# A transformer block's output projection: the gated bias put into the token tiles by ScalarE and the tokens added by the load, instead of additions on GpSimd

## The chip, the cores and the metric

One core of one Trainium2 chip. The metric is the device time of one execution in microseconds; the median of a few runs is given with the lowest and the highest.

## The reference

A conditioned transformer block (DiT block) on x of 2 batches x 2048 tokens x 512 channels, in float32. The condition gives six modulation vectors per batch (shift, scale and gate for the attention and for the MLP):

```
mod = silu(cond) @ Wada + bada;  sh_a, sc_a, gt_a, sh_m, sc_m, gt_m = split(mod, 6)
xm = layernorm(x; g1, be1) * (1 + sc_a) + sh_a
x  = x + gt_a * (causal_attention(xm; Wqkv, 16 heads of 32) @ Wproj + bproj)
xm = layernorm(x; g2, be2) * (1 + sc_m) + sh_m
x  = x + gt_m * (gelu(xm @ W1 + b1) @ W2 + b2)
```

The change concerns the third line: x + gt_a * (... @ Wproj + bproj). The kernel multiplies the gate into Wproj and into the bias ahead of time, so what is left is x + gated bias + (attention output @ gated Wproj).

## The kernel before, in words

The kernel runs in stages: keys, queries and values of batch 0; attention of batch 0; output projection of batch 0 (with the first steps of batch 1's normalisation beside it); the same three for batch 1 (with the first steps of the MLP beside the projection); then the MLP in four blocks of 512 tokens, taken two at a time. The matrix products of the linear layers use Strassen-like schemes of seven products, which is why there are many sums of blocks on VectorE and GpSimd.

The engines each have a queue of instructions and work through it in order. Most instructions around the projection are wrapped in `act(...)` or `mm(...)`, which keep them in program order on their engine; DMA issues on SP and a few others (the eviction in L1352 among them) are placed by the scheduler. An engine waits at the head of its queue, and all behind it wait with it.

**The output projection** is `project_phase` (L1302). It takes the 16 token tiles of 128 tokens of a batch in four quarters of 512 tokens, in the order `last_order` = 0, 2, 1, 3; I call the 16 tiles steps 0 to 15, and quarter k = 0 to 3. For each quarter the attention output lies transposed in a tile `at` of four chunks c0 to c3 of 128 channels; it has to be multiplied by the inverse softmax sums (`rbs`) before use. In a step:

- `tokens(n + 6)` makes sure that token tiles up to six ahead are being loaded (SP, L1318). The tiles of steps 0 to 3 were loaded during attention into space borrowed from a key tile (they show as `kst` in the profile), and the bias was added there by GpSimd (L472). The tiles of steps 4 to 15 are `xt`, with six buffers: tile 10 takes the buffer of tile 4, tile 11 that of tile 5, and so on, so a load waits until the store of the tile that had the buffer has read it.
- from quarter 1 on, GpSimd adds the gated bias `bgate` to the token tile (L1345).
- TensorE multiplies the four chunks of `at` by Wproj into a bank `ps_o` (L207 is the line of the helper for all matmuls; a step is 8 of them in the trace). All four chunks are needed for every token tile of the quarter.
- VectorE adds the bank to the token tile (L1352), takes the statistics for the second normalisation (L219, L222), and SP stores the tile as `x1d` (L1354).
- in the first three quarters, GpSimd scales one chunk of the next quarter's `at` (L1358): chunk c0 in the quarter's first step, c3 in its last. So the scalings of the third quarter are spread over steps 4 to 7, and step 8 needs all of them.
- `between(n)` does work for the next stage. In batch 0: statistics and normalisation of batch 1's first tokens (ScalarE L226 and L969, TensorE's transposes, ScalarE's evictions `xmT` in L279), the load of the weights `wqk` from GpSimd's queue (L931, after step 6), sums of them on VectorE and GpSimd (L949). In batch 1: the MLP's first normalisation (`xm`, half of its evictions on ScalarE, L279) and its token sums (L1637).

On SP also lie the loads of `at` (L1327), the path of the last softmax sums (`sum` store L745, `r` load L379, inverted on VectorE L386, `inv` store L387, wide load L393 into `rbs`), loads of pieces of W2 for sums made later (L1246), and in batch 1 the MLP's first weights (`w<-w1d`). The PSUM has six banks for the projection of batch 0 and four for that of batch 1, shared with the transposes.

Of the kernel before, what the change touches and what calls it, by code (L numbers as in the profile page):

```python
# [12 lines left out]
ALU = mybir.AluOpType  # L13
# [14 lines left out]
def dit_block_kernel(  # L28
# [36 lines left out]
    nc = tc.nc  # L65
# [6 lines left out]
    TQ = QB // P  # L72
# [11 lines left out]
    def pool(name, bufs=1, **kw):  # L84
        return tc.tile_pool(name=name, bufs=bufs, reuse_waits="tile", **kw)
# [68 lines left out]
    bgate = bp.tile([P, D], F32, tag="bgate", name="bgate")  # L154
# [46 lines left out]
    def x_rows(n):  # L201
        t0 = (n % NT) * P
        return x[n // NT, t0 : t0 + P, :]

    def mm(*args, **kw):

        return tc.keep_in_program_order(nc.tensor.matmul(*args, **kw))  # L207

    def act(ins):

        return tc.keep_in_program_order(ins)
# [5 lines left out]
    def stats(pool_, xt, n, mv, keep=False):  # L217
        st = pool_.tile([P, 6], F32, tag="stat", name="stat", bufs=2)
        ins = nc.vector.bn_stats(st, xt)  # L219
        if keep:  # L220
            act(ins)
        nc.vector.bn_aggr(mv[:, n, :], st)  # L222

    def inv_std(mv, rstd, shift, lo, hi, keep=False):
        order = act if keep else (lambda ins: ins)
        order(nc.scalar.activation(rstd[:, lo:hi], mv[:, lo:hi, 1], AF.Sqrt, bias=eps))  # L226
        order(nc.vector.reciprocal(rstd[:, lo:hi], rstd[:, lo:hi]))
        order(
            nc.vector.scalar_tensor_tensor(
                shift[:, lo:hi], mv[:, lo:hi, 0], -1.0, rstd[:, lo:hi],  # L230
                ALU.mult, ALU.mult,
            )
        )
# [1068 lines left out]
    def project_phase(row, psum, between):  # L1302

        b = row.b
        with pool(f"proj{b}") as pp:
            n = 0
            ats = list(row.at_s)  # L1310
            rbs = {1: row.rb_s[1], 2: row.old_queries(), 3: row.rb_s[0]}
            rows_x = [b * NT + i * TQ + t for i in last_order for t in range(TQ)]
            xts = list(row.xt_s)

            def tokens(upto):
                while len(xts) < min(upto, NT):
                    xt = pp.tile([P, D], F32, tag="xt", name="xt", bufs=6)
                    nc.sync.dma_start(xt, x_rows(rows_x[len(xts)]))  # L1318
                    xts.append(xt)

            row.load_sums(len(units) - 1, len(units))
            tokens(TQ + 6)
            for k, i in enumerate(last_order):
                if k in (0, 1):

                    at = pp.tile([P, C, QB], F32, tag="at", name="at", bufs=2)
                    nc.sync.dma_start(at, od[b][last_order[k + 2]])  # L1327
                    ats.append(at)
                at = ats[k]
                for t in range(TQ):  # L1330

                    if n == 0:
                        nc.sync.dma_start(rbs[2], wide_d[b][last_order[2]])
                        nc.sync.dma_start(
                            rbs[3][:, : C - 1], wide_d[b][last_order[3]][:, : C - 1]
                        )
                    elif n == 3:
                        row.invert(len(units) - 1, len(units))
                    elif n == 4:
                        row.widen(len(units) - 1, rbs[3][:, C - 1, :])  # L1340

                    tokens(n + 6)
                    nt, xt = rows_x[n], xts[n]
                    if k > 0:
                        act(nc.gpsimd.tensor_tensor(xt, xt, bgate, ALU.add))  # L1345
                    ps = psum.tile([P, D], F32, tag="mm", name="ps_o")
                    for c in range(C):
                        mm(
                            ps, at[:, c, t * P : (t + 1) * P], row.wproj[:, c, :],
                            start=(c == 0), stop=(c == C - 1),  # L1350
                        )
                    nc.vector.tensor_tensor(xt, ps, xt, ALU.add)  # L1352
                    stats(pp, xt, nt, mv2, True)
                    nc.sync.dma_start(x1d[nt], xt)  # L1354
                    if k + 1 < NQ:
                        d = ats[k + 1][:, t, :]
                        act(
                            nc.gpsimd.tensor_tensor(d, d, rbs[k + 1][:, t, :], ALU.mult)  # L1358
                        )
                    between(n)  # L1360
                    n += 1
        if b:
            inv_std(mv2, rstd2, shift2, NT, 2 * NT)
# [170 lines left out]
    with pool("qkv1") as qp, pool("ps_qkv1", bufs=6, space=PSUM) as ps_mm:  # L1534
# [3 lines left out]
        def between(n):  # L1538
            if n == 6:
                qkv.load_w(nc.gpsimd)  # L1540
            if 9 <= n < 12:
                qkv.weight_sum(nc.vector, n - 9)
            elif n == 13:
                qkv.weight_sum(nc.gpsimd, 3)
            if n >= 12:
                qkv.token_sum(0, (S1, S2, S3, A22)[n - 12])

            if n < MTT:
                qkv.stats(0, n, True)
            if n in (5, 8):  # L1550
                qkv.norm(0, n // 8)()
            if n == 8:
                qkv.load_x(1)
            if n >= NT - MTT:
                qkv.stats(1, n - (NT - MTT), True)

        project_phase(past, ps_mm, between)

        def also(g, n):
# [40 lines left out]
    with ExitStack() as mlp:  # L1600
# [104 lines left out]
        def between(n):  # L1705
# [10 lines left out]
            if n == 13:  # L1716
                for k in range(1, 5):
                    token_sum(k)

        project_phase(row, ps_mm, between)  # L1720
        for _ in range(3):
            next_weights()
# [814 lines left out]
```

## Time and profile before

| | |
|---|---|
| runs (3) | median 2240.48 us, 2238.31 to 2241.14 |
| profiled execution | 2238.97 us, its span 2237.2 us |
| granted TensorE clock | 0.999 |
| projection of batch 0 / batch 1 | from about 714 / 1458 us, some 57 to 60 us each |
| token loads (`xt<-in_x_dram`) | 12 in each, 256 KB each, from SP |
| additions of the bias (L1345) | 12 in each, on GpSimd |

In the rows of the profile PE is TensorE's matmuls, PEld its weight loads, DVE VectorE, ACT ScalarE, POOL GpSimd and SPq the issues of SP's DMA queue. A row of a timeline has the start, the duration, engine, line, operation, output<-input, shape and count, and in brackets how long the engine sat idle before and what released it. A row of a group has busy time, the mean in ns, then the idle time before and its releasers. A row of waits has the total, the number of waits and the longest.

### The profile page before, as it was taken

The page shows a single profiled execution, that of the slowest core. Times are in us where ns is not written, and L with a number is a line of the kernel's source. Part 1 is how long each engine was busy: PE and PEld are TensorE (multiplying, and loading weights), DVE is VectorE, ACT ScalarE, POOL GpSimd, SP SyncE. Part 2 cuts the span into 40 slices and gives each one's busy share as a digit, 9 for nine tenths or more (in the row PEclk, how much of TensorE's full clock was granted, in tenths as well). Part 3 has the DMA queues.
Part 4 walks back from the last instruction along what each step waited for, and adds up shares of the span by engine and source line. Part 5 has one row for each costly group of instructions (what it writes and reads, how often), then busy time and mean ns, then how long its engine had stood idle before and what let it go on. Part 6 is the DMA issues. An engine that isn't in the chain of part 4 may idle for free.

```text
span 2237.2 us, 34305 instructions
## 1 busy us (share of the span) xinstructions
PE 2196.1 (98%) x12273; PEld 1470.9 (66%) x12273; DVE 1580.7 (71%) x3373; ACT 1038.0 (46%) x2132; POOL 1458.9 (65%) x903
## 2 busy tenths in 40 slices
PE   7999999999999999999999999999999999999998
PEld 5887555555543588855555555345788888888887
DVE  4578766767757676777677777656586687688587
ACT  4444555655555244355655555703323532532520
POOL 4253998998992696189989898456616616535540
PEclk9999999999999999999999999999999999999999
DMA  8787143232233799542324113376655554654653
GB/s 273 249 278 192 42 89 76 67 86 48 88 111 114 258 311 317 153 105 62 86 67 104 35 52 127 105 243 216 236 181 177 192 173 157 212 183 142 219 158 111
DMA packets 166627, 340.99 MB, mean 152 GB/s; under 512 B 17216, under 2 KB 49516, under 8 KB 164664
## 3 DMA queue, kind: packets, MB, share of 16 engines
q1 hardware_dynamic: 158080, 302.05, 45.0%
q0 software_dynamic: 8000, 36.21, 4.3%
q8 instruction: 97, 1.59, 0.3%
q14 instruction: 74, 0.61, 0.1%
q10 hardware_dynamic: 376, 0.55, 0.1%
HBM read 246.46 MB, written 100.14 MB: 155 GB/s over the span
## 4 chain that ended last, share of the span: by engine, by line
PE 88%; DVE 4%; POOL 3%; DMA 2%; ACT 1%; issue 1%; SPq 0%; DVEq 0%; ACTq 0%; POOLq 0%
PE ps_a L207 23%; PE st L207 18%; PE ps_b L207 14%; PE o L207 10%; PE s L207 9%; PE ps_c L207 4%; PE ps_o L207 4%; PE sm L207 3%; DVE junk L503 1%; POOL ee L700 1%; PE ps_xt L215 1%; ACT e L675 1%; DVE mx L509 1%; PE ps_o L215 1%; POOL wqk L949 0%
## 5 line engine op out<-in xcount | busy, mean ns | idle before, releaser
L675 ACT ACTIVATE e<-st 128x512 f32<-128x512 f32 (+1 forms) x1152 | 574.7, 578 | 363.4 <-PE st L207 317.5
L509 DVE TENSOR_REDUCE mx<-s 128x1 f32<-128x512 f32 x576 | 381.7, 686 | 193.9 <-PE s L207 192.9
L700 POOL TENSOR_TENSOR ee<-ee,e 128x2048 f32<-128x2048 f32 x106 | 485.9, 4584 | 10.2 <-ACT e L675 4.3
L207 PE MATMUL st<-qst,kst 128*128 128x512 f32 (+3 forms) x1280 | 408.8, 386 | 0.0
L207 PE MATMUL s<-kst,qst 128*128 128x512 f32 (+3 forms) x1046 | 380.6, 395 | 6.0 <-DVE mx L509 3.7
L207 PE MATMUL ps_a<-sum,w 128*128 128x256 f32 (+1 forms) x1304 | 335.6, 391 | 3.1 <-DVE sum L1637 2.9
L207 PE MATMUL o<-e,vv 128*32 128x512 f32 (+3 forms) x2560 | 293.2, 537 | 0.3 <-POOL e L687 0.3
L207 PEld LDWEIGHTS st<-qst,kst 128*128 128x128 f32 x1280 | 228.5, 188 | 97.5 <-issue 65.7
L207 PEld LDWEIGHTS ps_a<-sum,w 128*128 128x128 f32 x1304 | 246.2, 190 | 44.3 <-issue 6.6
L503 DVE CUSTOM_DVE_ANT_0 junk<-s,causal 128x128 bf16<-128x128 f32 (+3 forms) x470 | 220.8, 470 | 61.2 <-PE s L207 47.4
L207 PEld LDWEIGHTS s<-kst,qst 128*128 128x128 f32 x1046 | 194.9, 188 | 71.0 <-DVE mx L509 17.0
L700 POOL TENSOR_TENSOR ee<-e 128x2048 f32<-128x2048 f32 x42 | 192.5, 4584 | 43.0 <-ACT e L675 43.0
L207 PE MATMUL ps_b<-sum,w 128*128 128x256 f32 (+1 forms) x744 | 186.8, 382 | 0.0
L2228 POOL TENSOR_TENSOR h<-h,h 128x512 f32<-128x512 f32 x96 | 119.4, 1274 | 69.8 <-DVE h L1734 69.8
L207 PEld LDWEIGHTS <-sel 32*128 32x128 bf16 x1152 | 29.6, 91 | 197.5 <-issue 196.6
L207 PEld LDWEIGHTS ps_b<-sum,w 128*128 128x128 f32 x744 | 140.4, 190 | 22.5 <-issue 2.6
L509 DVE TENSOR_REDUCE mx<-st 128x1 f32<-128x512 f32 x192 | 131.1, 683 | 0.5
L687 POOL TENSOR_SCALAR_AFFINE_SELECT e<-e 128x512 f32<-128x512 f32 x128 | 83.2, 669 | 68.1 <-ACT e L675 68.1
L1799 POOL TENSOR_TENSOR sum<-xm 128x256 f32<-128x256 f32 x22 | 23.2, 1054 | 154.3 <-PE ps_a L207 154.3
L207 PEld LDWEIGHTS o<-e,vv 128*32 128x32 f32 x2560 | 59.1, 108 | 92.3 <-issue 73.2
L207 PE MATMUL st<-fold,sel 32*128 32x512 bf16 (+1 forms) x1152 | 117.7, 372 | 1.4
L1071 POOL TENSOR_TENSOR lo<-lo,hi 128x512 fp32r<-128x512 f32 x32 | 40.7, 1274 | 105.7 <-ACT hi L1069 100.7
(263 smaller groups left out, 3580.4 us busy)
## 6 DMA issues: line engine op xcount, KB each, us to landing
w<-w1x SPq DMA_DIRECT2D x42, 896.0 KB
qst<-q SPq DMA_DIRECT2D x128, 256.0 KB
kst<-k SPq DMA_DIRECT2D x128, 256.0 KB
w<-w2d SPq DMA_DIRECT2D x28, 1024.0 KB
w<-w2d SPq DMA_DIRECT2D x28, 768.0 KB
q<-hi SPq DMA_DIRECT2D x32, 256.0 KB
q<-lo SPq DMA_DIRECT2D x32, 256.0 KB
k<-hi SPq DMA_DIRECT2D x32, 256.0 KB
```

The lines of the kernel that those rows point to most:

```text
L207: return tc.keep_in_program_order(nc.tensor.matmul(*args, **kw))
L215: return tc.keep_in_program_order(nc.tensor.transpose(dst, src, ident[:n, :n]))
L503: nc.vector.tensor_tensor_reduce(junk[:, :w], x, causal[:, QB - w :], 1.0, MASKED, ALU.add, ALU.max, m,)
L509: self.vector(nc.vector.tensor_reduce(m, x, axis=AX.X, op=ALU.max))
L675: act(nc.scalar.activation(e4[:, h, :w], sts[h][:, :w], AF.Exp))
L687: nc.gpsimd.affine_select(d, d, pattern=[[0, HC], [1, P]], compare_op=ALU.is_ge, fill=0.0, base=0, channel_multiplier=-1,)
L700: act(nc.gpsimd.tensor_tensor(dst, x, y, ALU.add))
L1071: engine.tensor_tensor(lo, d, hi.bitcast(F32), ALU.subtract)
L1799: act(engine.tensor_tensor(dst, u, v, ALU.subtract))
L2228: act(engine.tensor_tensor(d[j], d[j], x[j], ALU.add))
```

## The change

```
             def tokens(upto):
                 while len(xts) < min(upto, NT):
                     xt = pp.tile([P, D], F32, tag="xt", name="xt", bufs=6)
-                    nc.sync.dma_start(xt, x_rows(rows_x[len(xts)]))
+                    act(nc.scalar.copy(xt, bgate))
+                    act(
+                        nc.gpsimd.dma_start(
+                            xt, x_rows(rows_x[len(xts)]), accum_op=ALU.add
+                        )
+                    )
                     xts.append(xt)
 
             row.load_sums(len(units) - 1, len(units))
-            tokens(TQ + 6)
+            tokens(TQ + 4)
...
-                    tokens(n + 6)
+                    tokens(max(n + 4, TQ + 4))
                     nt, xt = rows_x[n], xts[n]
-                    if k > 0:
-                        act(nc.gpsimd.tensor_tensor(xt, xt, bgate, ALU.add))
```

A token tile of steps 4 to 15 is now made in two steps: ScalarE copies the gated bias into it, and a DMA issued from GpSimd's queue loads the tokens and adds them onto what is there. The addition on GpSimd goes, and so does the load from SP. Four tiles are started ahead of the first step, where six were, and in step n those up to tile n + 3 instead of n + 5. Copies and loads are kept in program order on ScalarE and on GpSimd. The order of instructions on TensorE and VectorE stays the same; on SP, the scheduler puts some DMAs in another order.

## The prediction

> **What bounds the kernel now.** I read the page first (busy time, chain), then the stretches of the two projections, then who TensorE waits for in them.
>
> ```profile
> PE 2196.1 (98%) x12273; PEld 1470.9 (66%) x12273; DVE 1580.7 (71%) x3373; ACT 1038.0 (46%) x2132; POOL 1458.9 (65%) x903
> ...
> PE 88%; DVE 4%; POOL 3%; DMA 2%; ACT 1%; issue 1%; SPq 0%; DVEq 0%; ACTq 0%; POOLq 0%
> ```
>
> TensorE is busy for 2196.1 of 2237.2 us, and 88% of the chain is TensorE. POOL's 65% says nothing yet: the changed stage has to be looked at by itself.
>
> ```profile
> 730.00:740.00 10.00, 10.00 (x31) 4.83 (x30) 5.19 (x13) 5.03 (x9) 6.03 (x5) 1.00 0.98 343
> 740.00:750.00 10.00, 9.66 (x29) 4.53 (x28) 5.60 (x11) 1.93 (x4) 9.98 (x11) 1.00 1.01 348
> ...
> 1475.00:1485.00 10.00, 10.00 (x37) 5.41 (x36) 6.87 (x12) 1.13 (x2) 9.84 (x8) 1.00 0.77 249
> ```
>
> The columns after the stretch are its length, then busy time of PE, PEld, DVE, ACT, POOL, then granted clock, DMA share and GB/s. In both projections TensorE is full at clock 1.00, even where POOL is full too (9.98, 9.84). ScalarE is nearly idle. One gap is left, 0.34 us in 740 to 750. The waits of TensorE from 700 to 800 and its timeline name it:
>
> ```profile
> PE ps_o L207 <- POOL at L1358: 0.3, 1, 0.3
> ```
> ```profile
> 742.56 2.74 PE L207 MATMUL ps_o<-kst,at 128*128 128x512 f32 x6
> 745.63 1.12 PE L207 MATMUL ps_o<-kst,at 128*128 128x512 f32 x2 [0.34 <-POOL at L1358]
> ```
>
> This is the first token tile (step 8 of 16, counting from 0) of the third quarter. It needs all four scaled chunks of its attention output, and GpSimd ends the fourth scaling only then. In the second projection TensorE waits for nothing. So the most that the change can remove here is 0.34 us of 2237.2, 0.015%; the question is what it can add. (About 0.2%, 4.5 us, is what a measurement of this kernel tells from no change.)
>
> **The change part by part.**
>
> *Removed: 24 additions on GpSimd, 24 loads from SP.*
>
> ```profile
> L1345 POOL TENSOR_TENSOR xt<-xt,bgate 128x512 f32<-128x512 f32 x24 | 32.1, 1339 | 30.8 <-DMA xt<-in_x_dram 20.6 <-DVE mv L222 4.7 <-DVE shift L229 2.6
> ```
> ```profile
>   POOL xt L1345: 10.3, 5
>   PE ps_o L207: 6.9, 3
> ```
>
> The first row is 24 x 1.339 = 32.1 us of GpSimd. The other two, from what VectorE sat idle for before it evicted the projection's banks in the first batch, say that VectorE waited 10.3 us for these additions. Both lie beside a full TensorE: six PSUM banks let VectorE lag. If that cover were gone, up to 10.3 us would be at stake; it is not gone, as the 0.34 us above is TensorE's only wait. Worth on the path: the addition between two scalings in the gap's chain, below.
>
> *Added on ScalarE: 24 copies of 128x512 from SBUF.* No such copy is in the trace; the bounds are the eviction copy (0.590) and the normalisation from SBUF (0.807).
>
> ```profile
> L744 ACT COPY sums<-sm 128x512 f32<-128x512 f32 x32 | 18.9, 590 | 8.6 <-PE sm L207 8.6
> L969 ACT ACTIVATE x<-x,shift,rstd 128x512 f32<-128x512 f32 x28 | 21.4, 807 | 6.2 <-DVE shift L229 5.1 <-ACT lo L1064 0.6 <-DMA q<-hi 0.6
> ```
>
> 24 x 0.59 to 0.81 = 14 to 19 us, on an engine busy 1.93 of 10 us in the stage. I take 0.7. What matters is the queue: from tile 10 on, the first that reuses one of the six buffers, a copy waits until the store out of that buffer has landed, and behind it on ScalarE stand the evictions of transposed tiles.
>
> *Added on GpSimd: 24 accumulating loads to issue.* The trace has no accumulating transfer. The nearest are plain issues on the same queue:
>
> ```profile
> L1278 POOL DMA_DIRECT2D w2d<-kst x10: 540/557/575, 796.8 to 887.4; - x10
> ```
> ```profile
> L931 POOL DMA_DIRECT2D wqk<-in_L_cond_Wqkv_dram x4: 722/731/790, 740.1 to 742.3; - x4
> ...
> DMA to landing us min/median/max: 6.3/8.7/10.5
> ```
> ```profile
> L1828 POOL DMA_DIRECT2D w1x<-w x4: 947/952/952, 1543.6 to 1594.5; - x4
> ```
>
> One run per partition costs 0.557, two 0.731, more 0.952. The new loads have one run per partition but a second operand: I take I = 0.73 and keep 0.55 to 0.95 (and, as a rival, far more). An addition of 1.27 thus gives way to about 0.73 on the same queue: GpSimd gains, unless an issue waits for its copy.
>
> *The chain at step 8.* GpSimd's order after the change is, by the compiled order of instructions: four loads, four scalings of the second quarter, scaling c0 of the third, load 8, c1, load 9, c2, four weight loads, load 10, c3. Rows of before:
>
> ```profile
> 736.01 1.90 ACT L279 ACTIVATE xmT<-ps_xt,c,a 128x256 f32<-128x256 f32 x4
> ```
> ```profile
> 738.89 1.27 POOL L1358 TENSOR_TENSOR at<-at,qst 128x512 f32<-128x512 f32 x1
> 740.10 2.96 POOL L931 DMA_DIRECT2D wqk<-in_L_cond_Wqkv_dram  x4
> 743.09 1.28 POOL L1345 TENSOR_TENSOR xt<-xt,bgate 128x512 f32<-128x512 f32 x1
> 744.30 1.27 POOL L1358 TENSOR_TENSOR at<-at,qst 128x512 f32<-128x512 f32 x1
> ```
>
> Copy 9 stands behind the four xmT evictions, which TensorE's transposes time, so it ends at 736.01 + 1.90 + 0.7 = 738.6. Then load 9 (I), c2 1.27, weights 2.96, load 10 (I), c3 1.27: 744.1 + 2I = 745.6 at I = 0.73. Before, c3 ended at 744.30 + 1.27 = 745.57. TensorE is ready at 742.56 + 2.74 = 745.30. So the gap stays: 0.0, with -0.34 at I = 0.55 and +0.4 at 0.95.
>
> *The store that copy 10 waits for.* SP's rows, and SP's own waits from 700 to 790:
>
> ```profile
> 736.64 0.43 SPq L1354 DMA_DIRECT2D x1d<-xt  x1
> ...
> 743.14 0.33 SPq L1318 DMA_DIRECT2D xt<-in_x_dram  x1
> 743.56 0.62 SPq L1354 DMA_DIRECT2D x1d<-xt  x1
> ...
> 752.16 0.34 SPq L1318 DMA_DIRECT2D xt<-in_x_dram  x1
> ```
> ```profile
> SPq L1318 <- DMA x1d<-xt: 21.4, 6, 6.4
> SPq L1246 <- POOL kst L1358: 10.6, 1, 10.6
> ```
> ```profile
> 731.65 0.69 DVE L1352 TENSOR_TENSOR xt<-ps_o,xt 128x512 f32<-128x512 f32 x1 [0.21 <-PE ps_o L207]
> ...
> 757.81 0.68 DVE L1352 TENSOR_TENSOR xt<-ps_o,xt 128x512 f32<-128x512 f32 x1
> ```
>
> Load 10 waited on SP for the store of tile 4, from 736.64 to 743.14, 6.5 us, and load 11 for that of tile 5, 8.6 us; now ScalarE waits. Load 10's turn on GpSimd comes at 738.6 + I + 1.27 + 2.96 = 743.6, so its copy must end by then and the store land by 742.9. The second wait helps: SP was held 10.6 us behind the scalings of the second quarter, because weights for the next stage stood ahead of the softmax sums. In the compiled order other weights go first, the sums leave up to 5 us earlier, and the store of tile 4, evicted at 732.3, can leave at about 733. It lands at 739.5 or, at 8.6, at 741.6: no wait. If it leaves as late as before, it lands at 743.1, the copy ends at 743.8, the load at 744.5 and c3 at 745.8, +0.2; at 8.6 us, +2.3.
>
> *Load 10 and its successors* queue behind the 2 MB of weights, which took up to 10.5 us: 744.3 + 10.5 = 755, against the eviction of tile 10 at 757.8 above. The later copies wait for stores of tiles 5 to 9, each due 3 us or more ahead. *The look-ahead* falls from 6 tiles to 4; tiles 8 and 9 have fresh buffers, so only the store wait comes of it. *Four loads ahead of the second quarter's scalings:*
>
> ```profile
> 714.27 0.59 ACT L744 COPY sums<-sm 128x512 f32<-128x512 f32 x1
> ```
> ```profile
> 713.49 4.93 POOL L1358 TENSOR_TENSOR kst<-kst,qst 128x512 f32<-128x512 f32 x4
> ```
> ```profile
> 714.11 20.87 PE L207 MATMUL ps_o<-kst 128*128 128x512 f32 x48
> ```
>
> Four copies end at 714.9 + 4 x 0.7 = 717.7, the last load at 718.4, the scalings 4.9 later, 723.3. A step is 8 of these matmuls, 3.45 us, so TensorE comes to step 4 at 727.9. Hidden by over 4 us.
>
> *The second projection.* The row that copy 9 stands behind, and step 8's start:
>
> ```profile
> 1482.15 0.56 ACT L279 ACTIVATE xm<-ps_xt,c,a 128x256 f32<-128x256 f32 x1 [0.42 <-DVE xm L274]
> ```
> ```profile
> 1488.27 13.90 PE L207 MATMUL ps_o<-kst,at 128*128 128x512 f32 x32
> ```
>
> Copy 9 ends at 1482.71 + 0.7 = 1483.4; load 9, c2, load 10 and c3 end at 1485.9 + 2I = 1487.4. The fourth chunk is due three quarters of a step after 1488.27, at 1490.9. 3.5 us to spare: nothing.
>
> *Sum:* 0.0 us (-0.34 to +2.3). The profiled execution is 2238.97 (span 2237.2, 1.8 around it); the median of the runs is 2240.48, 1.5 above. I predict the median unchanged: 2240.5, own range 2240.1 to 2242.8 before run spread.
>
> **The rivals.**
>
> *A, slower: the issue of an accumulating load is long.* The gap grows by 2I - 1.47. At I = 2.5 that is +3.5 at step 8; then four loads and four scalings stand between it and step 12, where scalings already stretched in the trace:
>
> ```profile
> 755.69 2.19 DVE L949 TENSOR_TENSOR wqk<-wqk 128x1024 f32<-128x1024 f32 x1
> ```
> ```profile
> 756.77 2.25 POOL L1358 TENSOR_TENSOR at<-at,qst 128x512 f32<-128x512 f32 x1
> ```
>
> A scaling took 2.25 rather than 1.27 beside VectorE's addition from SBUF. Steps 8 and 12 together give about +6: 2246.5. It decides from I = 2.2 (4.5 us); below 1 it is nothing. Against it: every issue in the rows is under 1 us. [...] The trace shows the stretching of scalings, but the plain issues at 740 had VectorE mostly idle beside them. [...] Chance 0.11.
>
> *B, slower: the accumulating transfer itself is slow.* A plain tile moves in 0.7 us by this row (36.21 MB in 4.3% of 2237 us is 376 GB/s):
>
> ```profile
> q0 software_dynamic: 8000, 36.21, 4.3%
> ```
>
> A read and a write of the destination would make it two or three times that. A step is 3.44 us, so it decides above about 4 us a tile; at 6, in order on one queue, the six tiles behind the weights (753) put tile 15 at 789. TensorE ends the stage near 771 and can run some 7 us further on its six banks, so it loses about 10, and as much in the second batch: +20, 2260. Nothing in the trace speaks for a factor of eight. Chance 0.05.
>
> *C, faster:* GpSimd's relief and SP's earlier stores remove more than the gap. TensorE's waits in the stage hold 0.34 us, so this needs later stages to shift as well; their orders of instructions are the same on all engines. 0.34 gives 2240.1, which cannot be told from no change; over 4.5 us, 2235, I can name no row for. Chance 0.05.
>
> *D, the change does nothing because the wait only moves:* GpSimd waits for ScalarE's copy, which waits for the store, as SP's load did. Beyond the forecast's end it goes if the store of tile 4 leaves 1.5 us later than before, behind the weights that now stand just ahead of it on SP, and takes 8.6: c3 ends at 749.4, +3.8, 2244.3. Chance 0.10, mostly within 0.2%.
>
> **How the numbers follow.** Forecast 0.69, A 0.11, B 0.05, C 0.05, D 0.10. Within 0.2%: 0.69 + 0.09 (D's part below 4.5 us) = 0.78; slower: A and B, 0.16, plus 0.01 of D, 0.17; faster 0.05. For 8 in 10 the range spans the runs' own spread below (2238.31) and reaches A's 2246.5 above; B is left out.
>
> **What would show it.** Right: TensorE's only wait in 700 to 800 still at step 8, 0 to 1 us, POOL's issues at 0.5 to 1 us, ScalarE's copies at 0.6 to 0.8 with idle time "<- DMA x1d" before some, SP free of its 10.6 us hold, VectorE's waits for POOL gone, the second projection full. Wrong: issues over 2 us; a tile landing over 10 us after its issue with VectorE waiting for it; a TensorE wait at step 12 or in 1458 to 1525; or the store of tile 4 landing after 745.

## The result and the profile after

| | before | after |
|---|---|---|
| median of 20 runs of each | 2237.93 us (2235.28 to 2241.84) | 2244.82 us (2239.80 to 2251.20) |
| ratio | | 1.0028, 95% interval 1.0020 to 1.0035 |
| profiled execution, its span | 2238.97, 2237.2 us | 2241.53, 2239.8 us |
| mean granted clock of the profiled execution | 0.999 | 0.999 |

The changed kernel is slower, by 6.3 us (4.5 to 7.8) going by the ratio. The profiled executions differ by 2.6 us only, so the profile shown first is one of the milder executions. That gap had to be explained too.

Page of after, engines and the queue of GpSimd's DMAs (packets, MB, share of 16 engines' time):

```profile
PE 2196.7 (98%) x12273; PEld 1469.9 (66%) x12273; DVE 1581.8 (71%) x3373; ACT 1050.9 (47%) x2156; POOL 1448.1 (65%) x903
...
q0 software_dynamic: 11456, 42.50, 6.0%
```

GpSimd is relieved by 10.8 us and ScalarE does 12.9 us more. Nothing in these totals speaks of a loss. It is in TensorE's waits of the two projections, from 700 to 800 and from 1455 to 1530 (total, times, longest):

```profile
PE ps_o L207 <- POOL at L1361: 1.0, 1, 1.0
PE ps_a L207 <- DVE lo L1083: 0.8, 1, 0.8
PE sm L207 <- DVE ee L703: 0.6, 1, 0.6
PE ps_xt L215 <- ACT qst L969: 0.4, 1, 0.4
```
```profile
PE ps_o L207 <- POOL at L1361: 1.7, 1, 1.7
PE sm L207 <- DVE ee L703: 0.6, 1, 0.6
```

The 0.6 us for sm lie ahead of the projections and stand in both lists of before too. Apart from the attention's last waits (sm, and one of 0.2 us), the lists of before held 0.34 us at step 8 of the first projection and none in the second. Now the largest is at step 8 of the second, where the prediction saw 3.5 us to spare. GpSimd, ScalarE and SP there:

```profile
1484.13 0.88 POOL L1320 DMA_DIRECT2D xt<-in_x_dram  x1 [10.06 <-ACT xt L1318]
1484.73 1.57 POOL L1361 TENSOR_TENSOR at<-at,qst 128x512 f32<-128x512 f32 x1
1491.17 0.88 POOL L1320 DMA_DIRECT2D xt<-in_x_dram  x1 [4.86 <-DVE xn L255]
1491.78 1.56 POOL L1361 TENSOR_TENSOR at<-at,qst 128x512 f32<-128x512 f32 x1
```
```profile
1483.22 0.61 ACT L1318 COPY xt<-bgate 128x512 f32<-128x512 f32 x1
1490.26 0.62 ACT L1318 COPY xt<-bgate 128x512 f32<-128x512 f32 x1 [6.42 <-DMA x1d<-xt]
```
```profile
1479.78 0.54 SPq L393 DMA_DIRECT2D qst<-inv  x1
...
1480.94 0.37 SPq L1664 DMA_DIRECT2D w<-w1d  x1
1481.41 0.60 SPq L1357 DMA_DIRECT2D x1d<-xt  x1
```

Read from the bottom: the store of tile 4 leaves SP at 1481.41, behind the inverse softmax sums (L393, held until they had landed) and an 896 KB load of MLP weights. ScalarE's copy 10 waits for it until 1490.26, 8.8 us after its issue. Load 10 follows at 1491.17 and scaling c3 stands behind it. (The page names VectorE's xn as releaser of load 10; that had long been done, and the copy ended at 1490.88.) VectorE had finished the store's tile at 1476.21 + 0.69 = 1476.9, so SP held the store for 4.5 us, and its landing took 8.8 us. Before, c3 came in a run of additions and scalings that nothing held, 11 us ahead of its need, and the store had left 5 us earlier. GpSimd and SP of before:

```profile
1478.48 1.27 POOL L1358 TENSOR_TENSOR at<-at,qst 128x512 f32<-128x512 f32 x1
```
```profile
1476.32 0.31 SPq L1354 DMA_DIRECT2D x1d<-xt  x1
```

**A length for each stage.** Times of whole runs scatter by several us (before's from 2235.28 to 2241.84), from causes outside the two projections too. So each profile below is read by the length of its two projections alone, from the start of the first ps_o matmul to that of the first matmul of the next stage. Rows of after:

```profile
714.37 16.15 PE L207 MATMUL ps_o<-kst 128*128 128x512 f32 x37
...
773.14 1.03 PE L207 MATMUL ps_a<-xmT,wqk 128*128 128x256 f32 x4
...
1458.74 17.43 PE L207 MATMUL ps_o<-kst 128*128 128x512 f32 x40
...
1520.14 1.88 PE L207 MATMUL ps_a<-xm,w 128*128 128x512 f32 x4
```

773.14 - 714.37 = 58.77 us and 1520.14 - 1458.74 = 61.40 us; before 57.39 and 59.43.

| kernel | first projection | second | ratio of times (95%) |
|---|---|---|---|
| before | 57.39 | 59.43 | |
| after | 58.77 | 61.40 | 1.0028 (1.0020 to 1.0035) |
| after, once more (e9) | 58.77 | 65.30 | 1.0035 (1.0022 to 1.0048) |
| eight buffers (e1) | 58.75 | 59.43 | 1.0013 (1.0004 to 1.0021) |
| scaling first (e2) | 57.90 | 59.43 | 1.0007 (0.9999 to 1.0016) |
| change in batch 0 alone (e3) | 58.74 | 59.43 | 1.0013 (1.0004 to 1.0021) |
| change in batch 1 alone (e4) | 57.57 | 65.14 | 1.0023 (1.0015 to 1.0032) |
| plain loads (e5) | 57.70 | 61.09 | 1.0004 (0.9995 to 1.0013) |
| copies alone (e6) | 57.83 | 59.43 | 1.0013 (0.9999 to 1.0026) |
| look-ahead of six (e7) | 69.72 | 70.20 | 1.0117 (1.0102 to 1.0132) |
| additions left out (e8) | 56.79 | 59.43 | 1.0004 (0.9995 to 1.0012) |
| held by 11 additions (e10) | 57.56 | 61.42 | 1.0010 (0.9998 to 1.0021) |
| held by 13 additions (e11) | 57.59 | 66.93 | 1.0034 (1.0021 to 1.0046) |
| both cures (e12) | 57.79 | 59.43 | 1.0008 (0.9997 to 1.0018) |

Where no GpSimd instruction is late the second projection lasts 59.43 us to the hundredth, so each excess there is the price of one stop (in e7, of several).

### The profile page after: what moved, and what is told of

Read it like the earlier page. It is cut to its first block, busy times and chain, and to the rows that moved or that the text cites. A ratio compares the mean times of both kernels' runs of the same rounds, so it can differ in the third digit from the quotient of the medians.

```text
span 2239.8 us, 34319 instructions
## 1 busy us (share of the span) xinstructions
PE 2196.7 (98%) x12273; PEld 1469.9 (66%) x12273; DVE 1581.8 (71%) x3373; ACT 1050.9 (47%) x2156; POOL 1448.1 (65%) x903
## 4 chain that ended last, share of the span: by engine, by line
PE 57%; DVE 2%; POOL 1%; DMA 1%; ACT 0%; issue 0%; SPq 0%; DVEq 0%; ACTq 0%; POOLq 0%
PE ps_a L207 19%; PE ps_b L207 11%; PE st L207 9%; PE o L207 5%; PE s L207 4%; PE ps_c L207 3%; PE ps_o L207 2%; PE sm L207 2%; PE ps_xt L215 1%; POOL ee L700 1%; PE ps_o L215 1%; DVE junk L503 1%; DVE mx L509 0%; DVE y L1737 0%; DVE sum L1640 0%
## 5 line engine op out<-in xcount | busy, mean ns | idle before, releaser
L1071 POOL TENSOR_TENSOR lo<-lo,hi 128x512 fp32r<-128x512 f32 x32 | 40.6, 1273 | 105.4 <-ACT hi L1069 105.3
```

What stands on the lines that cost most here:

```text
L1071: engine.tensor_tensor(lo, d, hi.bitcast(F32), ALU.subtract)
```

## The experiments

Theory W: the loss is the wait of scaling c3, on GpSimd, behind a load that waits through ScalarE's copy for the store of tile 4. Rivals A and B are those of the prediction: a price of each accumulating load, in its issue or in its transfer. Theory G comes from what e4 shows.

**e1, eight buffers.**

```
-                    xt = pp.tile([P, D], F32, tag="xt", name="xt", bufs=6)
+                    xt = pp.tile([P, D], F32, tag="xt", name="xt", bufs=8)
```

> Edit: the changed kernel with eight xt buffers instead of six. Tile 10 then has a buffer of its own, so neither its copy nor its load waits for the store of tile 4; issues, copies, accumulating transfers and all orders of instructions stay. Theory W (the scaling c3 of the third quarter stands on GpSimd behind a load that waits, through ScalarE's copy, for the landing of the store of tile 4): ScalarE's waits for x1d<-xt of 27.8 us mostly go, TensorE's wait at step 8 falls from 1.7 to 0 in the second projection and from 1.0 to at most 0.5 in the first; of the changed kernel's +6.3 us at least 4 go, ratio to the kernel before 1.0000 to 1.0010. Rival A (long issue of an accumulating load, and VectorE's and GpSimd's stretched instructions beside it): the issues are the same, +5 to +6 us stay, ratio 1.0022 or more. Rival B (slow accumulating transfer): the same +5 to +6 stay.

The second projection is back at 59.43 with the issues and the accumulating transfers as they were: its stop hung on that store, and A and B fall there. The first stays at 58.75, and its stop at 1.0 us:

```profile
PE ps_o L207 <- POOL at L1361: 1.0, 1, 1.0
```

So W is wrong for the first batch, and the ratio, 1.0013, misses the expected 1.0010: 3.4 of the 6.3 us went, not 4. What holds c3 in the first batch is told with the prediction's steps, below.

**e2, the scaling ahead of the next tile.**

```
-                    tokens(max(n + 4, TQ + 4))
...
                             nc.gpsimd.tensor_tensor(d, d, rbs[k + 1][:, t, :], ALU.mult)
                         )
+                    tokens(max(n + 4, TQ + 4))
                     between(n)
```

> Edit: the changed kernel with the start of the next token tile moved behind the scaling of the step, so on GpSimd c3 stands ahead of load 10 and not behind it. Six buffers, the copy still waits for the store. Theory W: TensorE's wait at step 8 goes in both projections (0 to 0.4 us), at least 4 of the 6.3 us go, ratio 1.0000 to 1.0010, although ScalarE's waits for x1d<-xt stay. Rival A: c3 ends one issue (0.9 us) earlier and nothing else changes: at most 1.8 us over the two batches, +4.5 stays, ratio about 1.0020. Rival B: the loads come a little later, +6 or more stays, ratio 1.0027 or more.

57.90 and 59.43, no wait at step 8 in either projection, ratio 1.0007: some 4.7 of the 6.3 us gone with copies, accumulating loads, buffers and the store's wait all as in the change. It is the place of c3 in GpSimd's queue that costs. A's 1.0020 and B's 1.0027 lie outside the interval.

**e3 and e4, one batch alone** (the other batch loads from SP and adds on GpSimd, as before).

```
+                    if b != 0:
+                        nc.sync.dma_start(xt, x_rows(rows_x[len(xts)]))
+                        xts.append(xt)
+                        continue
...
+                    if b != 0 and k > 0:
+                        act(nc.gpsimd.tensor_tensor(xt, xt, bgate, ALU.add))
```

> Edit: the change in the projection of batch 0 alone; batch 1 as in the kernel before. From the profiled pair (TensorE's wait at step 8 grew by 0.6 in batch 0 and by 1.7 in batch 1). Theory W, with the second store held longer behind other queue entries: about a quarter to a third of the loss, +1 to +2.5 us, ratio 1.0005 to 1.0011. Rivals A and B (a price of each load): half, +3.1 us, ratio 1.0014.

> Edit: the change in the projection of batch 1 alone; batch 0 as in the kernel before. Theory W: two thirds to three quarters of the loss, +3.8 to +5.3 us, ratio 1.0017 to 1.0024, with a wait of TensorE of 1.5 us or more at step 8 of the second projection. Rivals A and B: half, +3.1 us, ratio 1.0014.

1.0013 and 1.0023, together 1.0036: they add up (e3 lies a little above W's 1.0011), and batch 1 carries some two thirds, as W had it, although the intervals alone do not exclude halves. e4's profile brought what the first one of after lacked: a longer stop, and a slower TensorE behind it. Its timeline of TensorE, and then its ps_o matmuls from 1484 to 1500 (durations min, median, max):

```profile
1492.69 9.69 PE L207 MATMUL ps_o<-kst,at 128*128 128x512 f32 x18 [3.74 <-POOL at L1368]
```
```profile
L207 PE MATMUL ps_o<-kst,at x19: 592/592/1173, 1486.2 to 1499.6; 128*128 128x512 f32 x19
```

After a stop of 3.74 us matmuls take 1.17 us in place of 0.59, and the granted clock is 0.69, 0.50 and 0.95 in the three stretches of 2 us from 1492: (0.31 + 0.50 + 0.05) x 2 / 0.5 = 3.4 us at half clock. Around the stop of 1.7 us in the first profile of after it is 1.00 in all stretches from 1486 to 1500. This is theory G: a stop as long as e4's costs its length and a stretch at half clock behind it, one as short as that of after its length alone. It is the author's estimate from these two profiles.

**e5, plain loads.**

```
                         nc.gpsimd.dma_start(
-                            xt, x_rows(rows_x[len(xts)]), accum_op=ALU.add
+                            xt, x_rows(rows_x[len(xts)])
                         )
```

> Edit: the changed kernel with plain loads from GpSimd's queue in place of the accumulating ones; copies, waits, buffers and every order of instructions stay. The gated bias is thereby left out of the token tiles of steps 4 to 15. Theory W (the store that copy 10 waits for, and c3 queued behind): the issue falls from 0.90 us to 0.56 to 0.73, TensorE's waits at step 8 stay (0.3 to 1.0 us in the first projection, 1.5 to 4 in the second), +4 to +6.5 us stay, ratio 1.0018 to 1.0029. Rival B (the accumulating transfer or its issue is the price): most of the loss goes, at most +2 us, ratio below 1.0010.

Here W lost on the time: 1.0004, below its 1.0018. That is what rival B of this run expected (below 1.0010). Yet W's mechanism stands in the profile, a stop of 1.4 us in the second projection, of 61.09 us:

```profile
PE ps_o L207 <- POOL at L1361: 1.4, 1, 1.4
```

Going by the medians, the accumulation therefore counts for more than W allowed. What it adds is in these rows, of after and of e5, line L1320:

```profile
L1320 POOL DMA_DIRECT2D xt<-in_x_dram x24: 873/902/1867, 715.9 to 1508.4; - x24
...
DMA to landing us min/median/max: 4.0/6.5/11.3
```
```profile
L1320 POOL DMA_DIRECT2D xt<-in_x_dram x24: 537/577/590, 715.6 to 1506.7; - x24
...
DMA to landing us min/median/max: 3.0/4.6/9.4
```

and in the share of GpSimd's DMA queue from 1455 to 1500, of e4 and of e5:

```profile
q0 software_dynamic: 1264, 2.32, 30.6%
```
```profile
q0 software_dynamic: 720, 2.36, 16.7%
```

The issue is 0.90 us in place of 0.58, and the same bytes occupy the 16 DMA engines for 13.8 us in place of 7.5 (30.6% and 16.7% of 45 us), 1.8 times as long. The profiles hold only 1.4 of the some 5 us that e5 gains over after: 58.77 - 57.70 in the first projection and 61.40 - 61.09 in the second. That the transfer makes the store late they do not show: in e5 the inverse sums landed 7.4 us after their issue and the store of tile 4 after 9.0, in after 7.1 and 8.8. The rest of the gain lies in executions without a profile. That fewer of e5's runs have a long stop with half clock behind it (next runs) is suggested by their mean clock, 0.9992 over 11 runs against 0.9979 over 20 of after, though the clock varies for other reasons too (0.9983 in e2, which has no stop). How much of e5's gain is the issue and how much the transfer was not separated.

**e6, copies alone** (into a tile that nobody reads, in the kernel before).

```
                     nc.sync.dma_start(xt, x_rows(rows_x[len(xts)]))
+                    cb = pp.tile([P, D], F32, tag="cb", name="cb", bufs=2)
+                    act(nc.scalar.copy(cb, bgate))
```

> Edit: the kernel before, and beside each of its 24 token loads one copy of the gated bias on ScalarE into a tile that nobody reads: the copies alone, without the wait for a store. Theory W: nothing, ratio 0.9995 to 1.0005. Rival C1 (ScalarE's 24 copies of 0.62 us, or what they do to other engines' SBUF instructions, are a part of the loss): +1 us or more, ratio 1.0005 or more, with TensorE or VectorE waiting for ScalarE's evictions.

1.0013 lies in C1's range, above W's 1.0005, but its interval of 0.9999 to 1.0026 holds both and decides nothing. The stages do: 57.83 and 59.43, so 0.4 us in the first projection, where TensorE waits 0.77 us for GpSimd at step 8 instead of 0.34, and the second is untouched. In neither does TensorE wait for an eviction of ScalarE, which is what C1 needs.

**e7, a larger dose: the old look-ahead.**

```
-            tokens(TQ + 4)
+            tokens(TQ + 6)
...
-                    tokens(max(n + 4, TQ + 4))
+                    tokens(max(n + 6, TQ + 6))
```

> Edit: the changed kernel with the look-ahead of six tiles that the kernel before had (six started ahead, tiles up to n + 5 in step n), buffers still six. Now load 10 stands ahead of scaling c1 of the third quarter, load 11 ahead of c2 and load 12 ahead of c3, and tile 12's copy waits for the store of tile 6. Theory W, a larger dose: c3 ends when the store of tile 6, evicted at about 739 us, has landed 6.5 to 10 us later, plus copy, issue and scaling of about 2.5: 748 to 752 against a need at 745.3; TensorE waits 3 to 7 us at step 8 of each projection and later steps wait too, in all +8 to +20 us, ratio 1.0035 to 1.009. Rivals A and B (a price of each load): the loads are earlier and as many, no more than the changed kernel's +6.3, ratio at most 1.0028.

1.0117, 26 us: over W's 20, and four times what A and B allow. Three scalings now stand behind three such loads, and TensorE waits for them, in the first projection for 9.0 us in all:

```profile
PE ps_o L207 <- POOL at L1361: 9.0, 3, 4.0
```

The stages are 12.3 and 10.8 us longer. In the second, 3.8 us are waits for the scalings and 3.5 us a wait for an eviction (xm, L279) that stands on ScalarE behind a copy held by its store, so the late store reaches TensorE by ScalarE's queue too. The excess over the stops fits theory G: the clock was 0.59 from 750 to 760 and 0.66 from 1510 to 1520.

**e8, the additions left out.**

```
-                    if k > 0:
-                        act(nc.gpsimd.tensor_tensor(xt, xt, bgate, ALU.add))
```

> Edit: the kernel before without its 24 additions on GpSimd, loads from SP as they were: the removal alone, so the most that any way of moving these additions can bring. The gated bias is thereby left out of the token tiles of steps 4 to 15. Theory W with its side observation (GpSimd, relieved, starts its sums of W2 about 3 us earlier beside VectorE's addition L1071, which takes 2.9 us instead of 0.7 and holds TensorE 0.7 us at about 786 us): the 0.34 us at step 8 goes, up to 0.7 us come back later; ratio 0.9995 to 1.0005. Rival C (the additions hold more than TensorE's waits show): 2 us or more faster, ratio below 0.9991.

Even with the additions gone for nothing, the first projection is 0.6 us shorter (56.79), the second the same, and the time 1.0004 (0.9995 to 1.0012). That bounds what any change of this kind could bring here. The side observation fell: TensorE has no wait at 786 us in e8, although GpSimd starts its sums there even earlier (778.0). The addition L1071 beside them takes 1.61 us there and 2.96 in after, so the wait of 0.7 us comes from how the two fall on each other, not from the relief itself.

**e9, the changed kernel again.**

> The changed kernel itself once more, beside the next three on one chip: a second profiled execution, and a second median. [...]

1.0035 and a stop of 3.9 us, more than twice that of the first profile, of the same program. TensorE, then stretches of 2 us of all engines (length, busy time of PE, PEld, DVE, ACT and POOL, then granted clock, DMA share, GB/s):

```profile
1497.89 12.69 PE L207 MATMUL ps_o<-kst,at 128*128 128x512 f32 x25 [3.90 <-POOL at L1361]
```
```profile
1498.00:1500.00 2.00, 2.00 (x4) 0.90 (x5) 0.92 (x2) 0.10 (x1) 1.60 (x2) 0.77 1.04 347
1500.00:1502.00 2.00, 2.00 (x3) 0.67 (x2) 0.65 (x2) 0.62 (x1) 0.71 (x2) 0.50 1.08 226
1502.00:1504.00 2.00, 2.00 (x6) 0.93 (x5) 0.00 (x0) 0.62 (x1) 2.00 (x3) 0.88 0.69 156
```

At half clock for (0.23 + 0.50 + 0.12) x 2 / 0.5 = 3.4 us, that is 1.7 us of work lost. The stop, 3.9, and 1.7 make 5.6 of the stage's 5.87; the rest is about what e10's short stop, next, costs beyond its length (1.99 for 1.72). The mean clock of its 5 runs was 0.9970, against 0.9985 of the kernel before in the same rounds. So after's +6.3 is no fixed amount: the first projection and the wait at 787 us cost 1.4 + 0.7 in both profiles, the second projection 2.0 in one and 5.9 in the other: 4.1 or 8.0, with the 6.3 of the medians between. (The first profiled pair shows 2.6, as after's execution was shorter by 1.0 us between the projections.)

**e10 and e11, a stop made to measure** in the kernel before, with no copy and no accumulating load.

```
                         d = ats[k + 1][:, t, :]
+                        if b == 1 and n == 7:
+                            dm = pp.tile([P, D], F32, tag="dm", name="dm", bufs=1)
+                            for _ in range(11):
+                                act(nc.gpsimd.tensor_tensor(dm, bgate, bgate, ALU.add))
```

(13 in e11.)

> Edit: the kernel before with 11 additions into a tile that nobody reads, put on GpSimd ahead of scaling c3 of the third quarter in the second projection only: c3 ended at 1479.75 there and is due at 1491.0, so 11 x 1.23 = 13.5 us make TensorE wait about 2.2 us. No copies, no accumulating loads. Theory G (a short stop costs its own length, a long one more): +1.7 to +2.8 us, ratio 1.0008 to 1.0013, mean clock as before. Rival L (a stop costs its length whatever it is): the same.

> As the last, with 13 additions: 16.0 us, a stop of TensorE of about 4.7 us at step 8 of the second projection. Theory G: the stop and 1.5 to 2.0 us more from some 3.5 us at half clock, +6.2 to +7.0 us, ratio 1.0028 to 1.0031, mean granted clock lower by about 0.0008, matmuls of 1.17 us behind the stop. Rival L: its length alone, +4.7 us, ratio 1.0021, clock as before.

TensorE, and stretches of 2 us, of e10 and then of e11:

```profile
1491.43 11.43 PE L207 MATMUL ps_o<-kst,at 128*128 128x512 f32 x26 [1.72 <-POOL at L1362]
```
```profile
1492.00:1494.00 2.00, 2.00 (x6) 0.92 (x5) 1.30 (x2) 0.00 (x0) 2.00 (x3) 1.00 0.66 169
```
```profile
1491.88 14.49 PE L207 MATMUL ps_o<-kst,at 128*128 128x512 f32 x26 [4.17 <-POOL at L1362]
```
```profile
1490.00:1492.00 2.00, 0.12 (x1) 0.12 (x1) 0.00 (x0) 0.00 (x0) 2.00 (x3) 0.81 0.64 156
1492.00:1494.00 2.00, 2.00 (x3) 0.97 (x4) 0.00 (x0) 0.00 (x0) 2.00 (x2) 0.50 0.95 350
1494.00:1496.00 2.00, 2.00 (x3) 0.76 (x3) 1.57 (x3) 0.00 (x0) 2.00 (x3) 0.50 0.84 309
1496.00:1498.00 2.00, 2.00 (x3) 0.67 (x2) 0.00 (x0) 0.00 (x0) 2.00 (x3) 0.50 0.55 214
```

A stop of 1.72 us lengthened the stage by 1.99 and left the clock alone (1.00 in all stretches from 1484 to 1508); one of 4.17 lengthened it by 7.50, with half clock for 6.8 us. 2.45 us more of waiting cost 5.5 us. That is G against L in the profiles. The mean clock over all runs goes the same way, 0.9983 in e10 and 0.9975 in e11 against 0.9985 before. The times, 1.0010 and 1.0034, have intervals too wide to decide by themselves.

**e12, both cures.** The edits of e1 and e2 together.

> Edit: the changed kernel with eight buffers and with the start of the next tile moved behind the scaling, both cures together. Theory W: no wait at step 8 in either projection; what stays are the small waits of the first batch for stretched VectorE instructions (0.4 to 0.7 us before the transposes, 0.7 us at about 786 us), +0.5 to +1.5 us, ratio 1.0002 to 1.0007, no better than the kernel before, since that has 0.34 us to lose in these two stages. Rival A (a price of each accumulating load beside the waits): +2.5 us or more, ratio 1.0011 or more.

57.79 and 59.43, no wait at step 8, ratio 1.0008 (0.9997 to 1.0018), a little above W's 1.0007; the interval alone does not exclude A's 1.0011. In its stages the change costs then 0.4 us, and the 0.7 us at 786 us stays. No version of the change beats the kernel before, and by e8 there was 0.6 us to win.

## Why the prediction was right or wrong, point by point

**The bound: right.** TensorE is full and what can be removed is tiny: e8's first projection gains 0.6 us. That is 0.26 more than the wait of 0.34; e10's stop, too, cost 0.27 beyond its length (1.99 for 1.72).

**The failed step: "3.5 us to spare: nothing"** for the second projection. Its chain ran from copy 9 through load 9, c2 and load 10 to c3, as if load 10 could go at once. But the text itself had said that from tile 10 on a copy waits for the store out of its buffer, and this was worked out for the first batch only. In the second, SP's order puts that store behind the inverse sums and the weights; it left at 1481.41 and let copy 10 go at 1490.26. c3 ended at 1491.78 + 1.56 = 1493.3, against the forecast 1487.4. e1 and e2 show the step: each removes the stop by a cure of its own. Why the inverse sums landed so late was not tested; SP's new order issues them behind the 1 MB load of `at` (1472.64 and 1470.42; 7.1 us to land), where before they went ahead of it (1470.55 and 1473.26; 3.2 us).

**Rival D had the mechanism** (GpSimd waits for the copy, which waits for the store) and nearly the price, +3.8, but put it in the first batch, with a chance of 0.10. The sentence that TensorE's wait "in 1458 to 1525" would show the prediction wrong was the right one to watch.

**What was missing altogether: the price of a stop is not its length.** Every sum took a late microsecond of c3 for one microsecond. This case's profiles show a full clock (1.00) behind stops of 1.7 us (after, e10) and half clock (0.50) behind those of 3.7, 3.9 and 4.2 (e4, e9, e11).

**The step-8 chain of the first batch: a term mis-sized.** GpSimd of after:

```profile
739.85 0.89 POOL L1320 DMA_DIRECT2D xt<-in_x_dram  x1 [5.60 <-ACT xt L1318]
740.47 1.57 POOL L1361 TENSOR_TENSOR at<-at,qst 128x512 f32<-128x512 f32 x1
741.69 3.26 POOL L931 DMA_DIRECT2D wqk<-in_L_cond_Wqkv_dram  x4
744.65 1.27 POOL L1320 DMA_DIRECT2D xt<-in_x_dram  x1
745.27 1.95 POOL L1361 TENSOR_TENSOR at<-at,qst 128x512 f32<-128x512 f32 x1
```

The form of the sum holds: 739.85 to 747.22 is 7.37, and 2 x 0.90 + 2 x 1.27 + 2.96 is 7.30. But I is 0.90 and not 0.73 (a scaling right behind an issue shows 1.57 rather than 1.27: the next row starts while the issue still works), and copy 9 ended at 738.94 + 0.61 = 739.55 and not at 738.6, as the four evictions ahead of it came 1.1 us later:

```profile
737.15 1.90 ACT L279 ACTIVATE xmT<-ps_xt,c,a 128x256 f32<-128x256 f32 x4
738.94 0.61 ACT L1318 COPY xt<-bgate 128x512 f32<-128x512 f32 x1
```

VectorE's rows show why. ScalarE's normalisation ahead of those evictions waits for a small VectorE instruction, and this one took 1.09 us instead of 0.14 beside GpSimd's scaling c1 (732.67 to 734.25). Rows of before and of after:

```profile
732.99 0.14 DVE L229 SCALAR_TENSOR_TENSOR shift<-mv,rstd 128x4 f32<-128x4 f32 x1
```
```profile
733.18 1.09 DVE L229 SCALAR_TENSOR_TENSOR shift<-mv,rstd 128x4 f32<-128x4 f32 x1
```

No run isolates it. c3 ended at 747.22 and TensorE stood for 0.96 us. The range for the step (+0.4 at I = 0.95) was near; the start of the chain was taken as fixed.

**The store of tile 4 in the first batch**: "can leave at about 733" was wrong, it left at 736.85. It mattered little, since copy 10 ended at 743.2 and load 10 had its turn at 744.65; e1, where that wait is gone, has the same 58.75.

**Copies: right**, 0.62 us against 0.7; GpSimd's gain was real and worth nothing. **Rival A**: issues at 0.90 us (median; 0.87 to 1.87), below its 2.2; the 2.5 us in its sum no run shows. **Rival B**: the transfer costs 1.8 times a plain one, a little under the "two or three times" that the text held to be no harm, and VectorE waited for no tile. Where the transfer's part of the loss lies, if it has one beside the longer issue, stays open (e5).

**The chances.** "Within 0.2%" had 0.78, and the time came out 0.28% above the kernel before. The sum's own range (-0.34 to +2.3) does not hold these 6.3 us. The wider range does, but by luck: its upper end of 2246.5 was put there for A, whose long issue did not occur. Of the 0.69 for the forecast, the part for the second projection rested on one unexamined word, "nothing".

## What to carry to other kernels

When an operation is moved to another queue, list for that queue each instruction that will now stand behind it, and repeat the whole working for every place where the code runs: the same loop had 0 us to spare in one batch and 11 in the other, and the second lost more. A load that waits for a buffer belongs behind the work that is due, not ahead of it (e2 costs one line), or its buffer must be free by then (e1). Price a stop of TensorE by length and by what the clock does after it: here stops of 1.4 to 1.7 us cost 1.7 to 2.0, and stops of 3.7 to 4.2 us cost 5.7 to 7.5.

## What the runs showed of the hardware that was not expected

- Half clock came in stretches of 3.4 us (e9 and e4 above) and 6.8 us (e11). In e9 it began about 1.2 us after TensorE had resumed (0.77 in 1498 to 1500, against 1497.89), in e11 some 0.6 us before (0.81 in 1490 to 1492, against 1491.88). So in these two it does not begin with the end of the stop. Stops of 1.7 us (after, e10) had a clock of 1.00 behind them, stops of 3.7 to 4.2 us (e4, e9, e11) one of 0.50. From what length of stop on half clock follows, and what sets its start and its length, no run here shows.
- An accumulating load of 256 KB from GpSimd's queue took 0.90 us to issue and 6.5 us to land (median), a plain one 0.58 and 4.6, and the DMA engines were occupied 1.8 times as long by the same bytes.
- One VectorE addition of two operands from SBUF went from 0.69 to 2.96 us beside GpSimd's sums. VectorE of before and of after, then GpSimd of after:

```profile
780.62 0.69 DVE L1071 TENSOR_TENSOR lo<-lo,hi 128x512 fp32r<-128x512 f32 x1 [2.63 <-ACT hi L1069]
```
```profile
782.21 2.96 DVE L1071 TENSOR_TENSOR lo<-lo,hi 128x512 fp32r<-128x512 f32 x1 [2.56 <-ACT hi L1069]
```
```profile
782.09 1.30 POOL L1258 TENSOR_TENSOR qst<-kst 128x512 f32<-128x512 f32 x1
783.31 1.29 POOL L1258 TENSOR_TENSOR kst<-kst 128x512 f32<-128x512 f32 x1
```

  GpSimd's instructions kept their 1.3 us, and VectorE's started 0.12 us after one of them. In e8 it started 0.23 us after one (778.21 against 777.98) and took 1.61 us. The addition of 2.96 us is where after's 0.8 us at 787 us come from; what stretches it, no run isolates.
- Still open: in what share of executions the stop is long. The three profiles that have it (after, e9, e4) show 1.7, 3.9 and 3.7 us. In these three the inverse sums landed 7.1 to 8.6 us after their issue, against 3.2 before, and the store behind them 8.8 to 9.8 us after its own.
